# A gated recurrence over 512 steps: regrouping the recurrent product's PSUM banks, and dealing out the input products as 8, 8, 8, 4

## The chip, the core and the metric

The kernel runs on one core of a Trainium2 chip. The metric is the device time of one execution in microseconds (us), the median over several runs. Engines are named as in the profile: PE (TensorE, matmuls) and PEld (its loads of the stationary operand), DVE (VectorE), ACT (ScalarE), POOL (GpSimd), SP (SyncE, which issues DMAs).

## The reference, cut to what matters

```python
xT = jnp.swapaxes(x, 0, 1)                      # x: (8, 512, 512) = (batch, step, feature)

def step(h, x_t):                               # h: (8, 512)
    fused = jax.nn.sigmoid(jnp.concatenate([x_t, h], axis=-1) @ w_W + w_b)
    hidden_state, output_state = jnp.split(fused, 2, axis=-1)
    memory_state = x_t @ wx_W + wx_b + hidden_state * (h @ wh_W + wh_b)
    h_new = output_state * h + (1.0 - output_state) * jnp.tanh(memory_state)
    return (h_new, h_new)
_, hs = jax.lax.scan(step, h0, xT)
return x + jnp.swapaxes(hs, 0, 1)
```

Everything is float32. Each of the 512 steps multiplies the state of 8 x 512 numbers with 512 x 1536 weights: 512 columns for the gate `hidden_state` (called r in the kernel), 512 for `output_state` (z), and 512 for `h @ wh_W` (called h or hh). The input's share, x_t with 512 x 1536 weights too, doesn't depend on the state and can be made ahead.

## The kernel before

**Layout.** The state stands with the 512 features on partitions, in four chunks of 128 (k = 0 to 3). Chunks 0 and 1 are half A (tiles `hTA`), chunks 2 and 3 half B (`hTB`). In a matmul the state is the stationary operand, 32 columns wide (8 batch rows of the present step and 24 zeros), and the weights are the moving one. The output is 32 partitions high, so four matmuls with j = 0 to 3 stand side by side in the array, one to each group of 32 columns of it. The profile writes this as 128\*32. A float32 matmul of the program is two PE instructions.

**A step on PE.** Four steps are a group (`g = i // 4`, `s = i % 4`). The banks of PSUM, two sets of R, G and H, 128 columns each, are filled ahead with bias and input products, and the steps of a group add the recurrent product to 8 of 32 rows each. R holds r of both halves, G holds hh and z of half A, H holds z and hh of half B. The order is written out by hand (line 27): `R0 R1 G0 G1 R2 R3 G2 G3 H0 H1 H2 H3`. A unit such as R0 is the bank with the chunk k of the state, and it is four program matmuls, one for each j. Units with k = 0 and 1 need the new half A, those with k = 2 and 3 the new half B. What stands between two steps is input products (line 349).

**Input products.** Those of a pair of groups, eight steps, are 56 matmuls with 192 columns (`products`, line 288; they are 56, not 64, because sums of x and differences of weights are shared between the two groups). From step 5 on, every step takes seven of them after its H3. Since seven is not a multiple of four, three column groups get two and one gets one. `turn` (lines 343 and 350) carries on with the j that is next, so that the column group with one product is the first of the next step's R0, and each has its turn once in four steps. They run out with step 500: the last eleven steps have none.

**From PSUM to the next state** (lines 423 to 442), in DVE's order:

- `turn_r(0)`, `turn_r(1)`: transposes of R, 32x32 blocks, out of PSUM into `tr`; ACT makes r from each (`md0A`, `md0B`).
- `turn_h(0)`, `turn_z(0)`: the same for the two halves of G, into `md1A` and `tz`. `turn_z(0)` is made to wait for r of half A, so that the scans behind it need no wait of their own. ACT makes 1 - z (`hd0A`).
- `memory(0)`: two scans, one for each chunk of the half, make x_t wx + r (h wh) (`m`), and after each ACT makes tanh, into `hTA`.
- `update(0)`: two scans make the new half A (`hTA` of the next step), which PE waits for.
- `turn_h(1)`, `turn_z(1)`, `memory(1)`, `update(1)`: the same for half B, out of H.

After that follow, off this chain: copies of the state by ACT, `turn_x` (a transpose of the input's share for a later group), `spread` (ACT's copies of input products into a bank that is free), the copies and sums that finish the input products, three small memsets, and POOL's additions of x for the output, which SP stores after every 16 steps.

**Queues.** Each engine runs its instructions in the order in which the program issues them. On PE, the loads of stationary operands run ahead of the matmuls. The first load of R0, R1, R2 and R3 waits for DVE's scans.

Of the kernel before, what the change touches and what calls it, by code (L numbers as in the profile page):

```python
# [7 lines left out]
F32 = mybir.dt.float32  # L8
BF16 = mybir.dt.bfloat16
AF = mybir.ActivationFunctionType  # L10
ALU = mybir.AluOpType
PSUM = bass.MemoryType.PSUM

P = 128
NQ = 4
GS = 4
B = 8
HU = 64
# [5 lines left out]
LAST = 4  # L24
SYNC = mybir.DependencyInfo(mybir.DependencyClass.Sync, mybir.DependencyReason.DATA)

ORDER = "R0 R1 G0 G1 R2 R3 G2 G3 H0 H1 H2 H3"

FIRST = "Q0 x Q1 x Q2 x Q3 H0 H1 H2 H3"

BANKS = ("R", "G", "H")

HALF = 192

AL, BE = (0, slice(64, 256)), (0, slice(256, 448))
GA, DE = (1, slice(64, 256)), (1, slice(256, 448))

XP = {"G": slice(0, 128), "R": slice(128, 256), "X": slice(256, 384), "H": slice(384, 512)}


@with_exitstack
def tile_cond_rnn_residual(
# [2 lines left out]
    x: bass.AP,  # L45
    xh: bass.AP,
    wx_d: bass.AP,
    wgr_d: bass.AP,
    whh_d: bass.AP,
    wh3_d: bass.AP,  # L50
    bias_d: bass.AP,
    out: bass.AP,
    TC: int,
# [28 lines left out]
    nc = tc.nc  # L82
    NCH = x.shape[0]
    T = NCH * TC
    NG = T // GS
# [38 lines left out]
    for k in range(NQ):  # L124
        nc.sync.dma_start(out=wx[:, k], in_=wx_d[k])

    wgr = const.tile([P, NQ, NQ, 256], F32, name="wgr")
    for k in range(NQ):
        nc.sync.dma_start(out=wgr[:, k], in_=wgr_d[k])
    whh = const.tile([P, NQ, NQ, 128], F32, name="whh")  # L130
    nc.sync.dma_start(out=whh[:, :3], in_=whh_d)
    nc.sync.dma_start(out=whh[:, 3], in_=wh3_d)

    def wh(bank, k, j):
        return whh[:, k, j] if bank == "H" else wgr[:, k, j, {"G": slice(0, 128), "R": slice(128, 256), "Q": slice(0, 256)}[bank]]

    load_x(0, 1)

# [36 lines left out]
    def state(hf, i, slot=2):  # L175

        s = i % GS
        return hT[hf][i % NH][:, B * s : B * s + B, :, slot]

    ctx.enter_context(tc.manual_schedule())  # L180
    banks = [
        {n: psum.tile([P, 128], F32, name=f"{n}{q}") for n in BANKS}
        for q in range(2)
    ]
    xps = [psum.tile([P, 512], F32, name=f"xp{q}") for q in range(2)]
# [1 line left out]
    def mm(out_, lhsT, rhs, start=False):  # L187
        nc.tensor.matmul(  # L188
            out_, lhsT, rhs, start=start, stop=False, skip_group_check=True
        )  # L190


    for t_ in list(banks[0].values()) + list(banks[1].values()):
        mm(t_, none[:, :128], none, start=True)
    def warm():

        mm(xps[1], zeros[:, :128], zeros)
# [6 lines left out]
    for hf in range(2):  # L204
        for slot in (0, 2):
            nc.vector.tensor_copy(
                state(hf, 0, slot), hin[:, 2 * hf : 2 * hf + 2].rearrange("p c b -> p b c")
            )
    turn = [0]

# [2 lines left out]
    def act(key, out_, in_, func, **kw):  # L215
        inst = nc.scalar.activation(out_, in_, func, **kw).ins  # L216
        if key in written:
            tc.declare_no_dep(inst, written[key], reason="ordered through VectorE")
        written[key] = inst
        return inst  # L220
# [17 lines left out]
    def late(g):  # L238

        if g == 0:  # L240
            return xps[0][:, 256:512]
        return even if g % 2 == 0 else odd[g // 2 % 2]

    def spread(g, names):

        for n in names:
            src = late(g)[:, 128:256] if n == "H" else xps[g % 2][:, XP[n]]
            nc.scalar.copy(banks[g % 2][n], src)

    def turn_x(g, e):  # L250

        nc.vector.transpose(
            md1[e // 2][g % 2][:, :, e % 2, 1], late(g)[:, 32 * e : 32 * e + 32]
        )

    def reg(r):
        return xps[r[0]][:, r[1]]
# [47 lines left out]
    def take(it, n=None):  # L305
        while n is None or n > 0:
            if next(it, it) is it:
                return
            n = None if n is None else n - 1
# [9 lines left out]
    first = {g: prefill(g) for g in (1, 2, 3)}  # L319
    weight_sum(0)  # L320
    weight_sum(2)
    spread(0, "RGH")
    for e in range(NQ):
        turn_x(0, e)

# [1 line left out]
    for i in range(T):  # L327
# [7 lines left out]

        for n in (ORDER if i else FIRST).split():
            if n == "x":
                take(first[1], 1)
                continue
            bank, k = n[0], int(n[1])  # L340
            hs = hT[k // 2][i % NH][:, :, k % 2, 2]
            for j in range(NQ):
                j = (j + turn[0]) % NQ
                to = xps[0][:, :256] if bank == "Q" else ps[bank]
                mm(to[32 * j : 32 * j + 32, :], hs, wh(bank, k, j))
        if i < 5:
            take(first[(i + 3) // 2], 2)
        else:
            take(later, 7)
            turn[0] += 7  # L350

        rows = slice(B * s, B * s + B)

        def scans(hf, out_, d0, d1):

            for c_ in (slice(0, 1), slice(1, 2)):
                nc.vector.tensor_tensor_scan(  # L357
                    *[t_[:, :, c_].rearrange("p n c s -> p (n c s)") for t_ in (out_, d0, d1)],
                    0.0,
                    ALU.mult,  # L360
                    ALU.add,
                )
                yield c_

        if i:
            pg, pr = ps["G"], ps["R"]
        else:
            pg, pr = (xps[0][:, XP[n]] for n in "GR")
        raw = {
            "h": (pg[:, :HU], ps["H"][:, HU:]),  # L370
            "z": (pg[:, HU:], ps["H"][:, :HU]),
            "r": (pr[:, :HU], pr[:, HU:]),
        }

        def turned(n, hf):
            t_ = work.tile([P, 2, 32], F32, tag=f"t{n}{hf}", name=f"t{n}{hf}_{i}")
            inst = nc.vector.transpose(t_.rearrange("p c n -> p (c n)"), raw[n][hf]).ins  # L377
            return t_[:, :, rows], inst
# [1 line left out]
        r_done = [None, None]  # L380

        def turn_r(hf):
            tr, inst = turned("r", hf)

            if hf == 1 and i + 1 - NH in pool_done:
                tc.add_manual_dep(inst, pool_done[i + 1 - NH].name, SYNC)
            r_done[hf] = act(
                ("r", hf, g % 2, s),
                md0[hf][g % 2][:, rows, :, 1].rearrange("p n c -> p c n"),
                tr,  # L390
                AF.Sigmoid,
            )

        def turn_h(hf):
            nc.vector.transpose(  # L395
                md1[hf][g % 2][:, :, :, 0].rearrange("p n c -> p c n"), raw["h"][hf]
            )

        def turn_z(hf):
            tz, inst = turned("z", hf)  # L400

            tc.add_manual_dep(inst, r_done[hf].name, SYNC)
            act(
                ("zc", hf, i % 2),
                hd0[hf][i % 2][:, :, :, 2].rearrange("p n c -> p c n"),
                tz,
                AF.Sigmoid,
                scale=-1.0,
            )

        def memory(hf):

            m = work.tile([P, 2, B, 2], F32, tag=f"m{hf}", name=f"m{hf}_{i}").rearrange("p c n s -> p n c s")
            for c_ in scans(hf, m, md0[hf][g % 2][:, rows], md1[hf][g % 2][:, rows]):
                act(("n", hf, c_.start, i % NH), state(hf, i, 1)[:, :, c_], m[:, :, c_, 1], AF.Tanh)

        def update(hf):
            s1 = (i + 1) % GS
            new = hT[hf][(i + 1) % NH][:, B * s1 : B * s1 + B]
            for _ in scans(hf, new, hd0[hf][i % 2], hT[hf][i % NH][:, rows]):  # L420
                pass

        turn_r(0)
        turn_r(1)
        turn_h(0)
        turn_z(0)
        memory(0)
        update(0)
        if i == 0:

            seed(2)
        if i == T - 1:
# [3 lines left out]
                state(0, T),  # L436
                ALU.add,
            )
        turn_h(1)
        turn_z(1)  # L440
        memory(1)
        update(1)
        for hf in range(2):
            act(("h", hf, (i + 1) % NH), state(hf, i + 1, 0), state(hf, i + 1), AF.Copy)
        if i < 3:
# [3 lines left out]
        nxt, two = o + 1 < NG // 2, o + 2 < NG // 2  # L449
        if i == 0:  # L450
            nc.scalar.copy(odd[0], xps[1][:, 256:512])
        if g + 1 < NG:
            turn_x(g + 1, s)
        if i == 0:
            spread(1, "R")
        if u == 0:
            spread(2 * o + 1, "G")
            if o and nxt:
                nc.scalar.copy(reg(GA), reg(BE))
        elif u == 1:  # L460
            spread(2 * o + 1, "H")
        elif u == 2 and o == 0:
            seed(3)
            nc.scalar.copy(even, xps[0][:, 256:512])
        elif u == 2 and nxt:
            last = odd[(o + 1) % 2][:, :HALF]
            nc.vector.tensor_tensor(last, reg(GA), both, ALU.add)
        elif u == 3 and nxt:
            if o:
                nc.vector.tensor_tensor(even[:, :HALF], reg(BE), both, ALU.add)  # L470
            spread(2 * o + 2, "R")
        elif u == 4 and nxt:
            if o == 0:
                nc.scalar.copy(odd[1], xps[1][:, 256:512])
            spread(2 * o + 2, "G")
            if two:
                nc.scalar.copy(reg(AL), bias[:, AL[1]])
                x_sum(o + 2, 0)
        elif u == 5 and nxt:
            spread(2 * o + 2, "H")  # L480
            if two:
                nc.scalar.copy(reg(DE), step_bias)
                x_sum(o + 2, 1)
        elif u == 6 and two:
            nc.scalar.copy(reg(BE), reg(AL))
            x_sum(o + 2, 2)
        elif u == 7 and nxt:
            spread(2 * o + 3, "R")
            if two:
                nc.scalar.copy(both, reg(DE))  # L490
                x_sum(o + 2, 3)
# [104 lines left out]
```

## Time and profile before

| | us |
|---|---|
| median of 3 runs (lowest, highest) | 1681.29 (1680.15, 1682.52) |
| the profiled execution: its time | 1682.46 |
| the profiled execution: its span | 1679.9 |
| PE busy, PEld busy | 1668.8, 1645.4 |
| DVE busy, ACT busy, POOL busy | 1144.5, 947.4, 303.5 |
| granted PE clock, mean | 0.999 of full speed |

The span is what the profile covers; 2.6 us of the execution's time lie around it. A group of instructions is a row with line, engine, operation, what it writes and reads, its shape and its count, then its busy time and the mean of one in ns, then the idle time of its engine just before. A row of the timeline starts with the start in us from the beginning of the span and the length of the row, and several equal instructions that overlap stand in one row (x16). Line 188 is the helper `mm`, so PE's work is told apart by tiles. Matmuls overlap in the array, four at a time here, so PE's busy time has no gap where a single column group waits.

### The profile page before, as it was taken

What the parts mean: (1) busy time and instruction counts of PE and PEld (TensorE: products, weight loads), DVE (VectorE), ACT (ScalarE), POOL (GpSimd) and SP (SyncE); (2) the same over time, 40 slices, a digit from 0 to 9 for tenths busy, and PEclk for the clock granted to TensorE, in tenths of its full rate; (3) what the DMA queues carried; (4) which work ended last, traced back from release to release, by engine and by line L of the source; (5) the groups of instructions that cost most, each with busy time, mean ns of one, the idle gap of its engine ahead of it and who ended that gap; (6) DMA issues with size and microseconds to landing.
All of it is one profiled execution on the core that took longest, in us unless ns stands there. A gap on an engine that the chain in (4) does not pass through costs nothing.

```text
span 1679.9 us, 129621 instructions
## 1 busy us (share of the span) xinstructions
PE 1668.8 (99%) x56206; PEld 1645.4 (98%) x56206; DVE 1144.5 (68%) x9387; ACT 947.4 (56%) x5822; POOL 303.5 (18%) x1281
## 2 busy tenths in 40 slices
PE   8999999999999999999999999999999999999998
PEld 5999999999999999999999999999999999999997
DVE  6766666666666666666666666666666666666666
ACT  3555555555555555555555555555555555555554
POOL 1111111111111111111111111111111111111111
PEclk9999999999999999999999999999999999999999
DMA  4000000000000000000000000000000000000000
GB/s 178 17 5 17 18 18 17 17 5 18 17 18 18 5 17 18 17 17 5 18 18 17 18 15 7 18 17 17 17 5 18 17 18 17 5 18 12 11 11 10
DMA packets 11523, 31.37 MB, mean 19 GB/s; under 512 B 1220, under 2 KB 1732, under 8 KB 10952
## 3 DMA queue, kind: packets, MB, share of 16 engines
q1 hardware_dynamic: 10800, 22.94, 3.9%
q8 instruction: 439, 7.19, 1.7%
q14 instruction: 132, 1.08, 0.2%
q10 hardware_dynamic: 152, 0.16, 0.0%
HBM read 14.70 MB, written 8.39 MB: 14 GB/s over the span
## 4 chain that ended last, share of the span: by engine, by line
PE 99%; DVE 1%; DMA 0%; ACT 0%; issue 0%
PE R L188 27%; PE G L188 26%; PE H L188 26%; PE xp L188 19%; DMA rows<-in_bias_dram 0%; DVE md1A L395 0%; DVE hTA L357 0%; ACT hd0A L216 0%; DVE tz L377 0%; ACT hTA L216 0%; DVE bias L203 0%; DVE rows L120 0%; ACT hTB L216 0%; DVE hTB L357 0%; ACT hd0B L216 0%
## 5 line engine op out<-in xcount | busy, mean ns | idle before, releaser
L188 PE MATMUL R<-wgr,hTA 128*32 128x128 f32 x8176 | 431.5, 275 | 2.4 <-DVE hTA L357 2.2
L188 PE MATMUL G<-wgr,hTA 128*32 128x128 f32 x8176 | 411.9, 273 | 0.0
L377 DVE STREAM_TRANSPOSE tr<-R 128x64 f32<-128x64 f32 x1022 | 194.4, 228 | 286.9 <-PE R L188 286.8
L188 PE MATMUL R<-wgr,hTB 128*32 128x128 f32 x8176 | 385.9, 275 | 0.0
L499 POOL TENSOR_TENSOR ot<-xin,hTB 128x16 f32<-128x16 f32 x503 | 126.6, 252 | 1331.5 <-DVE hTB L357 1323.4
L188 PE MATMUL H<-whh,hTB 128*32 128x128 f32 x8192 | 366.4, 273 | 0.0
L188 PE MATMUL H<-whh,hTA 128*32 128x128 f32 x8192 | 366.2, 273 | 0.0
L188 PE MATMUL G<-wgr,hTB 128*32 128x128 f32 x8176 | 365.5, 273 | 0.0
L188 PEld LDWEIGHTS G<-wgr,hTA 128*32 128x32 f32 x8176 | 334.5, 122 | 0.2
L188 PEld LDWEIGHTS R<-wgr,hTA 128*32 128x32 f32 x8176 | 301.2, 123 | 9.0 <-DVE hTA L357 5.5
L188 PEld LDWEIGHTS H<-whh,hTB 128*32 128x32 f32 x8192 | 289.0, 122 | 0.1
L188 PEld LDWEIGHTS H<-whh,hTA 128*32 128x32 f32 x8192 | 289.0, 122 | 0.1
L188 PEld LDWEIGHTS G<-wgr,hTB 128*32 128x32 f32 x8176 | 288.6, 122 | 0.0
L216 ACT ACTIVATE hd0B<-tz 128x16 f32<-128x16 f32 x512 | 116.5, 228 | 279.4 <-DVE tz L377 279.3
L188 PEld LDWEIGHTS R<-wgr,hTB 128*32 128x32 f32 x8176 | 255.2, 123 | 2.2 <-DVE hTB L357 0.5
L216 ACT ACTIVATE md0A<-tr 128x16 f32<-128x16 f32 x512 | 112.0, 219 | 237.5 <-DVE tr L377 237.4
L188 PE MATMUL xp<-tw,sx 128*32 128x192 f32 x2976 | 229.3, 326 | 0.0
L357 DVE TENSOR_TENSOR_SCAN hTB<-hd0B,hTB 128x24 f32<-128x24 f32 x1024 | 158.0, 196 | 104.6 <-ACT hTB L216 104.4
L357 DVE TENSOR_TENSOR_SCAN hTA<-hd0A,hTA 128x24 f32<-128x24 f32 x1024 | 157.7, 195 | 103.2 <-ACT hTA L216 103.2
L188 PE MATMUL xp<-wx,xin 128*32 128x192 f32 (+1 forms) x2048 | 178.2, 331 | 0.4 <-issue 0.4
L216 ACT ACTIVATE hd0A<-tz 128x16 f32<-128x16 f32 x512 | 115.7, 226 | 111.1 <-DVE tz L377 111.1
L216 ACT ACTIVATE hTB<-hTB 128x16 f32<-128x16 f32 x512 | 120.4, 235 | 79.6 <-DVE hTB L357 70.9
(90 smaller groups left out, 2408.9 us busy)
## 6 DMA issues: line engine op xcount, KB each, us to landing
xin<-in_x_dram SPq DMA_DIRECT2D x31, 256.0 KB, 3.5
out_dram<-ot SPq DMA_DIRECT2D x31, 256.0 KB, 2.2
wx<-in_wx_dram SPq DMA_DIRECT2D x4, 768.0 KB, 7.0
wgr<-in_wgr_dram SPq DMA_DIRECT2D x4, 512.0 KB, 9.7
whh<-in_whh_dram SPq DMA_DIRECT2D x1, 768.0 KB
whh<-in_wh_dram SPq DMA_DIRECT2D x1, 256.0 KB, 10.9
out_dram<-ot SPq DMA_DIRECT2D x1, 192.0 KB, 1.8
head<-in_xh_dram ACTq DMA_DIRECT2D x1, 144.0 KB, 5.0
```

Of the source, the lines that this page charges most:

```text
L188: nc.tensor.matmul(out_, lhsT, rhs, start=start, stop=False, skip_group_check=True)
L216: inst = nc.scalar.activation(out_, in_, func, **kw).ins
L357: nc.vector.tensor_tensor_scan(*[t_[:, :, c_].rearrange("p n c s -> p (n c s)") for t_ in (out_, d0, d1)], 0.0, ALU.mult, ALU.add,)
L377: inst = nc.vector.transpose(t_.rearrange("p c n -> p (c n)"), raw[n][hf]).ins
L499: return engine.tensor_tensor(ot[:, t, 2 * hf : 2 * hf + 2, :].rearrange("p c n -> p n c"), x_of(c, slice(2 * hf, 2 * hf + 2), t, 1).rearr ...
```

## The change

The banks are now A (192 columns: hh, z and r of half A), B (128: r and hh of half B) and C (64: z of half B). The order of a step becomes `A0 B0 A1 A2 A3 B1 B2 B3 C0 C1 C2 C3`. `turn` is gone; a step takes eight input products, and only four if it is the first of its group. On DVE, `turn_r(1)`, `turn_h(1)` and `turn_z(1)` move in between the scans of half A, and the second `update` of half A comes after them; it waits for r of half B. What waited for POOL's additions was `turn_r(1)`, and is now `turn_h(0)`. `turn_x` runs up to four steps later and reads partly from PSUM. The columns of the weights and of `wx` are regrouped to fit, in the host's code and in the loads: `wa` (four loads of 384 KB) and `wb` (one of 1152 KB and one of 384 KB) in place of `wgr` (four of 512 KB) and `whh` (768 and 256 KB).

```diff
-ORDER = "R0 R1 G0 G1 R2 R3 G2 G3 H0 H1 H2 H3"
-FIRST = "Q0 x Q1 x Q2 x Q3 H0 H1 H2 H3"
-BANKS = ("R", "G", "H")
+ORDER = "A0 B0 A1 A2 A3 B1 B2 B3 C0 C1 C2 C3"
+FIRST = "A0 x A1 x A2 x A3 B0 B1 B2 B3 C0 C1 C2 C3"
+BANKS = {"A": 192, "B": 128, "C": 64}
...
-XP = {"G": slice(0, 128), "R": slice(128, 256), "X": slice(256, 384), "H": slice(384, 512)}
+XP = {"A": slice(0, 192), "X": slice(192, 320), "C": slice(320, 384), "B": slice(384, 512)}
...
+    def part(g, c0, c1):
+        return late(g)[:, c0 - 256 : c1 - 256] if c0 >= 256 else xps[g % 2][:, c0:c1]
     def spread(g, names):
         for n in names:
-            src = late(g)[:, 128:256] if n == "H" else xps[g % 2][:, XP[n]]
-            nc.scalar.copy(banks[g % 2][n], src)
+            nc.scalar.copy(banks[g % 2][n], part(g, XP[n].start, XP[n].stop))
     def turn_x(g, e):
-        nc.vector.transpose(
-            md1[e // 2][g % 2][:, :, e % 2, 1], late(g)[:, 32 * e : 32 * e + 32]
-        )
+        c0 = XP["X"].start + 32 * e
+        nc.vector.transpose(md1[e // 2][g % 2][:, :, e % 2, 1], part(g, c0, c0 + 32))
...
             for j in range(NQ):
-                j = (j + turn[0]) % NQ
-                to = xps[0][:, :256] if bank == "Q" else ps[bank]
+                to = ps[bank] if i or bank != "A" else xps[0][:, XP["A"]]
                 mm(to[32 * j : 32 * j + 32, :], hs, wh(bank, k, j))
         if i < 5:
             take(first[(i + 3) // 2], 2)
         else:
-            take(later, 7)
-            turn[0] += 7
+            take(later, 8 if s else 4)
...
         raw = {
-            "h": (pg[:, :HU], ps["H"][:, HU:]),
-            "z": (pg[:, HU:], ps["H"][:, :HU]),
-            "r": (pr[:, :HU], pr[:, HU:]),
+            "h": (pa[:, :HU], ps["B"][:, HU:]),
+            "z": (pa[:, HU : 2 * HU], ps["C"]),
+            "r": (pa[:, 2 * HU :], ps["B"][:, :HU]),
         }
...
         def turn_z(hf):
             tz, inst = turned("z", hf)
-            tc.add_manual_dep(inst, r_done[hf].name, SYNC)
+            if hf == 0:
+                tc.add_manual_dep(inst, r_done[0].name, SYNC)
...
         turn_r(0)
-        turn_r(1)
         turn_h(0)
         turn_z(0)
-        memory(0)
-        update(0)
+        memory(0, 0)
+        memory(0, 1)
+        turn_r(1)
+        update(0, 0)
+        turn_h(1)
+        turn_z(1)
+        tc.add_manual_dep(update(0, 1), r_done[1].name, SYNC)
...
-        turn_h(1)
-        turn_z(1)
-        memory(1)
-        update(1)
+        memory(1, 0)
+        memory(1, 1)
+        update(1, 0)
+        update(1, 1)
...
-        if g + 1 < NG:
-            turn_x(g + 1, s)
+        ahead = 2 * o + (1 if u < 3 else 2 if u < 7 else 3)
+        if ahead < NG:
+            turn_x(ahead, (u + 1) % GS)
         if u == 0:
-            spread(2 * o + 1, "G")
+            spread(2 * o + 1, "B")
...
```

In the calls of `spread`, R, G and H become A, B and C step for step.

More of the change, by code (lines that the diff above doesn't have):

```diff
@@ L47, in tile_cond_rnn_residual @@
     wx_d: bass.AP,
-    wgr_d: bass.AP,
-    whh_d: bass.AP,
-    wh3_d: bass.AP,
+    wa_d: bass.AP,
+    wb_d: bass.AP,
+    wb3_d: bass.AP,
     bias_d: bass.AP,
@@ L125, in tile_cond_rnn_residual @@
         nc.sync.dma_start(out=wx[:, k], in_=wx_d[k])
-    wgr = const.tile([P, NQ, NQ, 256], F32, name="wgr")
+    wa = const.tile([P, NQ, NQ, 192], F32, name="wa")
     for k in range(NQ):
[L129 to L132, printed above, removed]
+        nc.sync.dma_start(out=wa[:, k], in_=wa_d[k])
+    wb = const.tile([P, NQ, NQ, 192], F32, name="wb")
+    nc.sync.dma_start(out=wb[:, :3], in_=wb_d)
+    nc.sync.dma_start(out=wb[:, 3], in_=wb3_d)
     def wh(bank, k, j):
-        return whh[:, k, j] if bank == "H" else wgr[:, k, j, {"G": slice(0, 128), "R": slice(128, 256), "Q": slice(0, 256)}[bank]]
+        return wa[:, k, j] if bank == "A" else wb[:, k, j, {"C": slice(0, 64), "B": slice(64, 192)}[bank]]
     load_x(0, 1)
@@ L181, in tile_cond_rnn_residual @@
     banks = [
-        {n: psum.tile([P, 128], F32, name=f"{n}{q}") for n in BANKS}
+        {n: psum.tile([P, w], F32, name=f"{n}{q}") for n, w in BANKS.items()}
         for q in range(2)
@@ L193, in tile_cond_rnn_residual @@
     for t_ in list(banks[0].values()) + list(banks[1].values()):
-        mm(t_, none[:, :128], none, start=True)
+        mm(t_, none, none[:, :1].broadcast_to([P, t_.shape[1]]), start=True)
     def warm():
@@ L208, in tile_cond_rnn_residual @@
             )
-    turn = [0]
     written = {}
@@ L321, in tile_cond_rnn_residual @@
     weight_sum(2)
-    spread(0, "RGH")
+    spread(0, "BCA")
     for e in range(NQ):
@@ L348, in tile_cond_rnn_residual, with scan @@
         else:
-            take(later, 7)
-            turn[0] += 7
+            take(later, 8 if s else 4)
         rows = slice(B * s, B * s + B)
[L354 to L368, printed above, removed]
+        def scan(c_, out_, d0, d1):
+            return nc.vector.tensor_tensor_scan(
+                *[t_[:, :, c_].rearrange("p n c s -> p (n c s)") for t_ in (out_, d0, d1)],
+                0.0,
+                ALU.mult,
+                ALU.add,
+            ).ins
+        pa = ps["A"] if i else xps[0][:, XP["A"]]
         raw = {
-            "h": (pg[:, :HU], ps["H"][:, HU:]),
-            "z": (pg[:, HU:], ps["H"][:, :HU]),
-            "r": (pr[:, :HU], pr[:, HU:]),
+            "h": (pa[:, :HU], ps["B"][:, HU:]),
+            "z": (pa[:, HU : 2 * HU], ps["C"]),
+            "r": (pa[:, 2 * HU :], ps["B"][:, :HU]),
         }
@@ L382, in turn_r @@
         def turn_r(hf):
-            tr, inst = turned("r", hf)
-            if hf == 1 and i + 1 - NH in pool_done:
-                tc.add_manual_dep(inst, pool_done[i + 1 - NH].name, SYNC)
+            tr, _ = turned("r", hf)
             r_done[hf] = act(
@@ L394, in turn_h @@
         def turn_h(hf):
-            nc.vector.transpose(
+            inst = nc.vector.transpose(
                 md1[hf][g % 2][:, :, :, 0].rearrange("p n c -> p c n"), raw["h"][hf]
-            )
+            ).ins
+            if hf == 0 and i + 1 - NH in pool_done:
+                tc.add_manual_dep(inst, pool_done[i + 1 - NH].name, SYNC)
         def turn_z(hf):
             tz, inst = turned("z", hf)
-            tc.add_manual_dep(inst, r_done[hf].name, SYNC)
+            if hf == 0:
+                tc.add_manual_dep(inst, r_done[0].name, SYNC)
             act(
@@ L409, in turn_z, with memory, update @@
             )
[L411 to L417, printed above, removed]
+        ms = [
+            work.tile([P, 2, B, 2], F32, tag=f"m{hf}", name=f"m{hf}_{i}").rearrange("p c n s -> p n c s")
+            for hf in range(2)
+        ]
+        def memory(hf, q):
+            c_ = slice(q, q + 1)
+            scan(c_, ms[hf], md0[hf][g % 2][:, rows], md1[hf][g % 2][:, rows])
+            act(("n", hf, q, i % NH), state(hf, i, 1)[:, :, c_], ms[hf][:, :, c_, 1], AF.Tanh)
+        def update(hf, q):
             s1 = (i + 1) % GS
             new = hT[hf][(i + 1) % NH][:, B * s1 : B * s1 + B]
-            for _ in scans(hf, new, hd0[hf][i % 2], hT[hf][i % NH][:, rows]):
-                pass
+            return scan(slice(q, q + 1), new, hd0[hf][i % 2], hT[hf][i % NH][:, rows])
         turn_r(0)
-        turn_r(1)
         turn_h(0)
         turn_z(0)
-        memory(0)
-        update(0)
+        memory(0, 0)
[5 more added lines that the diff above has]
+        tc.add_manual_dep(update(0, 1), r_done[1].name, SYNC)
         if i == 0:
@@ L451, in tile_cond_rnn_residual @@
             nc.scalar.copy(odd[0], xps[1][:, 256:512])
-        if g + 1 < NG:
-            turn_x(g + 1, s)
-        if i == 0:
-            spread(1, "R")
+            spread(1, "A")
+            turn_x(1, 0)
+        ahead = 2 * o + (1 if u < 3 else 2 if u < 7 else 3)
+        if ahead < NG:
+            turn_x(ahead, (u + 1) % GS)
         if u == 0:
-            spread(2 * o + 1, "G")
+            spread(2 * o + 1, "B")
             if o and nxt:
@@ L460, in tile_cond_rnn_residual @@
         elif u == 1:
-            spread(2 * o + 1, "H")
+            spread(2 * o + 1, "C")
         elif u == 2 and o == 0:
@@ L470, in tile_cond_rnn_residual @@
                 nc.vector.tensor_tensor(even[:, :HALF], reg(BE), both, ALU.add)
-            spread(2 * o + 2, "R")
+            spread(2 * o + 2, "A")
         elif u == 4 and nxt:
@@ L474, in tile_cond_rnn_residual @@
                 nc.scalar.copy(odd[1], xps[1][:, 256:512])
-            spread(2 * o + 2, "G")
+            spread(2 * o + 2, "B")
             if two:
@@ L479, in tile_cond_rnn_residual @@
         elif u == 5 and nxt:
-            spread(2 * o + 2, "H")
+            spread(2 * o + 2, "C")
             if two:
@@ L487, in tile_cond_rnn_residual @@
         elif u == 7 and nxt:
-            spread(2 * o + 3, "R")
+            spread(2 * o + 3, "A")
             if two:
@@ L551 @@
     w, wxm, whm = f["L0_cond_w_W"], f["L0_cond_wx_W"], f["L0_cond_wh_W"]
-    wb, wxb, whb = f["L0_cond_w_b"], f["L0_cond_wx_b"], f["L0_cond_wh_b"]
+    wb_, wxb, whb = f["L0_cond_w_b"], f["L0_cond_wx_b"], f["L0_cond_wh_b"]
     def quads(a):
@@ L565, in chunks @@
         return c_(units(a).swapaxes(0, 1))
-    wx_d = chunks(cat((z[:D], half_a), (r[:D], both), (wxm, both), (z[:D], half_b)))
-    wgr_d = chunks(cat((whm, half_a), (z[D:], half_a), (r[D:], both)))
-    wh = units(cat((z[D:], half_b), (whm, half_b)))
-    whh_d, wh3_d = c_(wh[:, :3]), c_(wh[:, 3])
-    rb, zb = wb[:512], wb[512:]
-    bias_d = c_(cat((whb, half_a), (zb, half_a), (rb, both), (wxb, both), (zb, half_b), (whb, half_b))[0])
+    wx_d = chunks(cat((z[:D], half_a), (r[:D], half_a), (wxm, both), (z[:D], half_b), (r[:D], half_b)))
+    wa_d = chunks(cat((whm, half_a), (z[D:], half_a), (r[D:], half_a)))
+    wb = units(cat((z[D:], half_b), (r[D:], half_b), (whm, half_b)))
+    wb_d, wb3_d = c_(wb[:, :3]), c_(wb[:, 3])
+    rb, zb = wb_[:512], wb_[512:]
+    bias_d = c_(
+        cat((whb, half_a), (zb, half_a), (rb, half_a), (wxb, both), (zb, half_b), (rb, half_b), (whb, half_b))[0]
+    )
     xd = units(_np.moveaxis(x, 2, 0))
@@ L582 @@
     for name, a in (
-        ("x", xd), ("xh", xh_d), ("wx", wx_d), ("wgr", wgr_d), ("whh", whh_d), ("wh3", wh3_d), ("bias", bias_d),
+        ("x", xd), ("xh", xh_d), ("wx", wx_d), ("wa", wa_d), ("wb", wb_d), ("wb3", wb3_d), ("bias", bias_d),
     ):
```

## The prediction

> **What bounds the kernel now.** I read the page first.
>
> ```profile
> span 1679.9 us, 129621 instructions
> PE 1668.8 (99%) x56206; PEld 1645.4 (98%) x56206; DVE 1144.5 (68%) x9387; ACT 947.4 (56%) x5822; POOL 303.5 (18%) x1281
> ...
> PE 99%; DVE 1%; DMA 0%; ACT 0%; issue 0%
> ```
>
> PE never stands still as a whole, but four column groups work in it, and one can wait unseen. So I went to the timeline of the last steps, which have no input products, and where the chain from PSUM to the next state lies bare. One step, on DVE:
>
> ```profile
> 1655.62 0.38 DVE L377 STREAM_TRANSPOSE tr<-R 128x64 f32<-128x64 f32 x2 [0.55 <-PE R L188]
> 1656.06 0.25 DVE L395 STREAM_TRANSPOSE md1A<-G 128x64 f32<-128x64 f32 x1
> 1656.23 0.21 DVE L377 STREAM_TRANSPOSE tz<-G 128x64 f32<-128x64 f32 x1
> 1656.36 0.26 DVE L357 TENSOR_TENSOR_SCAN m<-md0A,md1A 128x16 f32<-128x16 f32 x2
> 1656.82 0.31 DVE L357 TENSOR_TENSOR_SCAN hTA<-hd0A,hTA 128x24 f32<-128x24 f32 x2 [0.20 <-ACT hTA L216]
> 1657.05 0.22 DVE L395 STREAM_TRANSPOSE md1B<-H 128x64 f32<-128x64 f32 x1
> 1657.20 0.20 DVE L377 STREAM_TRANSPOSE tz<-H 128x64 f32<-128x64 f32 x1
> ...
> 1659.21 0.25 DVE L395 STREAM_TRANSPOSE md1A<-G 128x64 f32<-128x64 f32 x1
> ```
>
> on ACT (r, 1 - z, tanh of half A):
>
> ```profile
> 1655.90 0.22 ACT L216 ACTIVATE md0A<-tr 128x16 f32<-128x16 f32 x1 [0.53 <-DVE tr L377]
> ...
> 1656.47 0.23 ACT L216 ACTIVATE hd0A<-tz 128x16 f32<-128x16 f32 x1 [0.22 <-DVE tz L377]
> 1656.60 0.29 ACT L216 ACTIVATE hTA<-m 128x8 f32<-128x8 f32 x2
> ```
>
> and on PE, with the loads of R's first units:
>
> ```profile
> 1657.09 0.66 PE L188 MATMUL R<-wgr,hTA 128*32 128x128 f32 x16 [0.22 <-DVE hTA L357]
> ...
> 1658.53 0.62 PE L188 MATMUL G<-wgr,hTB 128*32 128x128 f32 x16
> 1658.96 0.62 PE L188 MATMUL H<-whh,hTA 128*32 128x128 f32 x16
> ```
> ```profile
> 1657.08 0.19 PEld L188 LDWEIGHTS R<-wgr,hTA 128*32 128x32 f32 x8 [0.48 <-DVE hTA L357]
> ```
>
> To be seen: without input products the loop takes 1659.21 - 1656.06 = 3.15 us; half A's scan starts at 1656.82, PE's loads 0.26 later; and R's row is 0.66 long where G's is 0.62, so a load that had to wait costs 0.04. With products I count turns of G:
>
> ```profile
> L395 DVE STREAM_TRANSPOSE md1A<-G 128x64 f32<-128x64 f32 x464 | 117.8, 254 | 26.1
> L188 PE MATMUL xp<-tw,sx 128*32 128x192 f32 x2976 | 229.3, 326 | 0.0
> L188 PE MATMUL G<-wgr,hTA 128*32 128x128 f32 x8176 | 411.9, 273 | 0.0
> ```
>
> The first row is of the window from 100 to 1600 us: 1500 / 464 = 3.233 us a step, 12.93 for four.
>
> **PE's share, in us.** Sixteen instructions (two units) start 0.43 to 0.44 apart (1658.53, 1658.96), four in each column group: 0.109 each. 192 columns last 326 - 273 = 0.053 longer: 0.162. A unit is two instructions in each column group, so 0.218 with 128 columns and 0.325 with 192. Twelve units make 2.62; a product adds 0.325 to its column group.
>
> Before, a column group thus needs 2.62 + 0.65 = 3.27 in three steps of four, and 2.95 in the one in which it gets one product and leads. There it waits for the loop. I take the 3.15 to 3.16 of the tail less 0.04, since there all four column groups start again late and apart, and here one. 3 x 3.27 + 3.12 = 12.93, as counted. So the kernel is bound by PE in three steps of four, and by the loop in the fourth; without any wait four steps would take 4 x 2.62 + 28 / 4 x 0.325 = 12.76.
>
> **The change, part by part.**
>
> *Widths.* The columns are the same: 4 x 0.325 + 4 x 0.218 + 4 x 0.112 = 2.62. The 0.112 for C is a straight line downwards, 0.109 - 0.053 = 0.056 an instruction; no row has 64 columns. Bounds: 0.056, and 0.109 if a narrow one cost what 128 columns do. I take 0.056: a waiting load costs 0.04 (R's 0.66 against 0.62), less than 0.056, and eight loads fit into 0.19 with 0.12 for each (mean 123 ns), (0.19 - 0.12) / 7 = 0.01 apart; C needs one every 0.014. The Trainium skill speaks against it: "TensorE: Matmul & The Clock Gate", section "LDWEIGHTS (loading the stationary operand)", has a load last its columns over 1.2 GHz, 27 ns for 32. One after another, that would make C's 32 loads a step 0.85 instead of 0.45, and the time some 0.4 x 500 = 200 us longer. The loads 0.01 apart in the row above speak for loads that overlap, and my sum goes without it.
>
> *Products.* 28 in four steps as before. All column groups now get two, or all get one: PE asks for 3.27, 3.27, 3.27 and 2.95, and no column group runs ahead.
>
> *Half A's chain.* Time 0 is the start of B1 in the last column group, where A ends. A's last instruction still has 0.273 - 0.109 = 0.16 to run, and DVE starts 0.04 to 0.06 later (in the tail G ends at 1658.53 + 0.62 = 1659.15 and its turn starts at 1659.21): `turn_r(0)` at 0.20 to 0.23. r was ready early; now r, hh and z end together, and `turn_z(0)` must wait for ACT's r: 0.28 (1655.62 to 1655.90) + 0.22 + 0.03 from ACT to DVE (tanh from 1656.60, 0.20 long, scan at 1656.82) = 0.53, where two transposes alone would take 0.17 each. From there as before: z's turn to half A's first scan is 1656.82 - 1656.23 = 0.59, and to the loads 0.26. Loads at 0.20 + 0.53 + 0.85 = 1.58 to 1.61, matmul 0.04 later: 1.62 to 1.65.
> PE gets to A0 after B1 to B3, C and products: 3 x 0.218 + 0.447 + 0.65 = 1.75, the first column group 0.02 earlier. No wait there. With four products it gets there at 1.43, and waits about 0.2.
>
> *Half B's chain.* After half A's first scan (0.20 + 1.12 = 1.32 to 1.35): `turn_h(1)` + 0.10 (1656.82, a second scan 0.13 later, 1657.05), `turn_z(1)` + 0.15, second scan + 0.13, m's scan + 0.10 to 0.13, tanh + 0.21 (m's mean of 0.17 and 0.03 to 0.04 to ACT), scan + 0.23, loads + 0.26. Sum 1.18 to 1.21: loads at 2.50 to 2.56, matmul at 2.54 to 2.60, last column group 0.02 later. If z's turn takes longer after standing idle (the two turns of `tr` last 0.38 with starts 0.17 apart: 0.25 for a first, 0.21 for the second), 0.04 more: 2.56 to 2.66 in all. PE gets to A2 at 1.75 + 0.325 + 0.218 + 0.325 = 2.62. With A2 and A3 (0.65) the next time 0 comes at 3.27 to 3.31 in a step with eight, and at 3.21 to 3.31 in one with four, where PE alone would need 2.95. Four steps: 13.02 to 13.24, against 12.93: + 0.09 to 0.31. With the loop in the middle, 3.26, they take 3 x 3.27 + 3.26 = 13.07; as a loop above 3.27 lengthens all four steps and one below it only one, I take 13.09, + 0.16.
>
> *Ends.* Steps 5 to 500 are 124 times four: + 11 to 38 us, taken + 20. The last eleven pay 0.06 to 0.16 each: + 1 to 2. The first five have 384-column products that hide all this.
>
> *Costed at nothing.* `spread` copies the same columns, `turn_x` moves within DVE's order, the wait for POOL is for an addition seven steps old; DVE idles 0.55 a step before `tr`, ACT 0.53, and that is their cover; without it each would cost its 0.19 to 0.27 in the step concerned. `turn_r(1)` falls into DVE's idle 0.20 before half A's scans, and B's bank is done by then (0.65 + 0.2 = 0.85, asked for at 1.05); so is C's (about 1.3, asked for at 1.57). B0 and C0 wait for turns that are over by 1.9, and start after 1.95. SP's loads for step 0: 5.6 MB instead of 5.8 stand ahead of B0; below 0.5 once.
>
> Sum: 1682.46 (the profiled execution, span 1679.9 and 2.6 around it) + 21 = 1704. The median shown is 1.2 lower, which makes **1703**.
>
> **Rivals.**
>
> *Faster: the end of A comes earlier.* A is done after 4 x 0.325 + 0.218 = 1.52 of a step, G was after 8 x 0.218 = 1.75. If r stayed off the path (z's turn 0.35 behind r's, not 0.53), both loads come 0.18 earlier, a step with four takes 3.03 to 3.13 and four steps 12.84 to 12.94, 12.89 in the middle: 1681 - 5 = 1676. With no wait anywhere, 12.76: 1681 - 21 = 1660. It decides from 12.93 = 9.81 + 3.12: the loop has to be under 3.12. For it: the 0.23 are real. Against: m's scan needs r whatever the order, and r's 0.53 is in the rows.
>
> *Slower by far: narrow matmuls.* If C's instructions cost 0.109, every step pays 8 x 0.053 = 0.42, also behind the loop's waits in most: 3 x 3.70 + 3.37 = 14.47, + 191 us, about 1873. It leaves the main case's range from 0.063 an instruction on (3 x 8 x 0.007 x 124 = 21 on top of 1703). For it: no row has 64 columns. Against: the loads.
>
> *No change.* Should the step with four take 3.12 by other small savings, 1681.
>
> **How the numbers follow.** Main case 0.78; faster 0.10; none 0.04; narrow matmuls 0.08. This kernel's three runs lie within 0.07% of their median, so 0.2% tells a change. Main case's range is 1693 to 1721 (+ 12 to + 40 on 1681); the rivals outside it hold 0.2, and the range given is 1690 to 1722. Slower: 0.78 + 0.08 = 0.86.
>
> **What would show it.** The turn of A's r, once a step: intervals of 3.27 to 3.31 in three and 3.21 to 3.31 in the fourth. ACT's r ahead of z's turn in every step, DVE idle for about 0.2 between `turn_h(0)` and `turn_z(0)`. PE idle, or its A0 waiting for `hTA`, only behind four products. C's 32 instructions within 0.45. I am wrong if four steps take under 12.93, if the step with four takes under 3.12, or if C takes 0.5 or more.

## The result and the profile after

The changed kernel takes 1720.37 us (median of 4 runs, 1719.41 to 1723.04) against 1681.9 before: a ratio of 1.0231, 95% interval 1.0213 to 1.0249. It is slower, as forecast, and near the far end of the range: 38 us more where 21 were taken. The profiled execution took 1723.04 us, 1720.5 of them in its span. From its page (a group's last numbers are busy time, mean ns of one, and the engine's idle time ahead of them):

```profile
span 1720.5 us, 129875 instructions
PE 1698.3 (99%) x56238; PEld 1414.3 (82%) x56238; DVE 1126.3 (65%) x9387; ACT 959.0 (56%) x5822; POOL 303.1 (18%) x1281
...
PE 88%; DVE 6%; ACT 4%; issue 1%; DMA 0%
...
L188 PEld LDWEIGHTS A<-wa,hTB 128*32 128x32 f32 x8176 | 243.6, 125 | 111.5 <-DVE hTB L355 92.3
...
L371 DVE STREAM_TRANSPOSE tz<-A 128x64 f32<-128x64 f32 x511 | 128.0, 251 | 79.0 <-ACT md0A L215 75.9
```

PE's busy share is 99% in both kernels, because one matmul or another is always under way. What tells them apart is the loads, busy for 82% of the span instead of 98%, and the chain that ended last, which before was PE to 99% and now goes through DVE and ACT too. Of the idle time of the loads, 92.3 us are laid to half B's scan, ahead of A2. z's turn waits 76 us for ACT's r.

One step on DVE in the changed kernel's timeline:

```profile
808.10 0.25 DVE L371 STREAM_TRANSPOSE tr<-A 128x64 f32<-128x64 f32 x1 [0.76 <-PE A L188]
808.28 0.21 DVE L386 STREAM_TRANSPOSE md1A<-A 128x64 f32<-128x64 f32 x1
808.64 0.25 DVE L371 STREAM_TRANSPOSE tz<-A 128x64 f32<-128x64 f32 x1 [0.16 <-ACT md0A L215]
...
809.27 0.21 DVE L355 TENSOR_TENSOR_SCAN hTA<-hd0A,hTA 128x24 f32<-128x24 f32 x1
...
810.20 0.31 DVE L355 TENSOR_TENSOR_SCAN hTB<-hd0B,hTB 128x24 f32<-128x24 f32 x2 [0.19 <-ACT hTB L215]
...
811.41 0.25 DVE L371 STREAM_TRANSPOSE tr<-A 128x64 f32<-128x64 f32 x1 [0.76 <-PE A L188]
```

and on PE and its loads:

```profile
808.51 0.41 PE L188 MATMUL C<-wb,hTA 128*32 128x64 f32 x16
808.73 0.41 PE L188 MATMUL C<-wb,hTB 128*32 128x64 f32 x16
808.95 0.83 PE L188 MATMUL xp<-wx,xin 128*32 128x192 f32 x16
...
810.47 0.87 PE L188 MATMUL A<-wa,hTB 128*32 128x192 f32 x16
```
```profile
810.47 0.51 PEld L188 LDWEIGHTS A<-wa,hTB 128*32 128x32 f32 x16 [0.17 <-DVE hTB L355]
```

The loop is 811.41 - 808.10 = 3.31 us. It goes 0.54 from r's turn to z's, 0.63 to half A's scan, 1.20 to the loads for A2, and 0.94 from there over A2 and A3 to the next turn. This step has eight products (the sixteen instructions at 808.95) and is no exception. The table has the median interval between one step's turn and the next one's, by the step that it starts from, over steps 13 to 490, and in the last steps, where there are no products; the turn is that of hh of half A. It holds most of the runs told of below, too.

| us | after s = 0 | s = 1 | s = 2 | s = 3 | last steps |
|---|---|---|---|---|---|
| before | 3.247 | 3.252 | 3.253 | 3.207 | 3.158 |
| changed | 3.309 | 3.306 | 3.308 | 3.307 | 3.302 |
| changed, r of A from a constant | 3.006 | 3.270 | 3.270 | 3.270 | 3.007 |
| changed, seven products a step | 3.308 | 3.305 | 3.305 | 3.305 | 3.303 |
| changed, wait on r ahead of the scan | 3.152 | 3.271 | 3.271 | 3.270 | 3.150 |
| before, with 8, 8, 8, 4 | 3.162 | 3.270 | 3.270 | 3.270 | 3.157 |
| before, z with r first | 3.233 | 3.253 | 3.249 | 3.219 | 3.148 |
| before, hh with r first, z last | 3.239 | 3.245 | 3.189 | 3.242 | 3.068 |

In the changed kernel all steps take the same, with eight products, four or none. PE binds none of them.

### The profile page after: what moved, and what is told of

The parts are those of the page before. It is cut to its first block, busy times and chain, and to the rows that moved or that the text cites. A ratio compares the mean times of both kernels' runs of the same rounds, so it can differ in the third digit from the quotient of the medians.

```text
span 1720.5 us, 129875 instructions
## 1 busy us (share of the span) xinstructions
PE 1698.3 (99%) x56238; PEld 1414.3 (82%) x56238; DVE 1126.3 (65%) x9387; ACT 959.0 (56%) x5822; POOL 303.1 (18%) x1281
## 4 chain that ended last, share of the span: by engine, by line
PE 88%; DVE 6%; ACT 4%; issue 1%; DMA 0%
PE A L188 42%; PE B L188 21%; PE xp L188 15%; PE C L188 10%; DVE tz L371 2%; DVE tr L371 2%; ACT md0A L215 2%; ACT hd0A L215 2%; DVE hTA L355 2%; ACT hTA L215 1%; DMA rows<-in_bias_dram 0%; DVE bias L203 0%; ACT hTB L215 0%; ACT xp L223 0%; DVE rows L120 0%
## 5 line engine op out<-in xcount | busy, mean ns | idle before, releaser
L188 PE MATMUL A<-wa,hTA 128*32 128x192 f32 x8176 | 527.3, 329 | 13.3 <-DVE hTA L355 4.0
L188 PE MATMUL A<-wa,hTB 128*32 128x192 f32 x8176 | 446.2, 335 | 0.2 <-DVE hTB L355 0.2
L188 PE MATMUL B<-wb,hTA 128*32 128x128 f32 x8192 | 414.0, 273 | 0.0
L188 PEld LDWEIGHTS A<-wa,hTB 128*32 128x32 f32 x8176 | 243.6, 125 | 111.5 <-DVE hTB L355 92.3
L188 PEld LDWEIGHTS B<-wb,hTA 128*32 128x32 f32 x8192 | 292.8, 121 | 40.9
L188 PEld LDWEIGHTS A<-wa,hTA 128*32 128x32 f32 x8176 | 236.2, 123 | 109.4 <-DVE hTA L355 61.6
L188 PE MATMUL B<-wb,hTB 128*32 128x128 f32 x8192 | 318.7, 273 | 0.0
L188 PEld LDWEIGHTS B<-wb,hTB 128*32 128x32 f32 x8192 | 241.4, 122 | 0.0
L188 PE MATMUL C<-wb,hTA 128*32 128x64 f32 x8192 | 209.4, 219 | 0.0
L188 PE MATMUL C<-wb,hTB 128*32 128x64 f32 x8192 | 209.3, 219 | 0.0
```

The lines of the kernel that those rows point to most:

```text
L188: nc.tensor.matmul(out_, lhsT, rhs, start=start, stop=False, skip_group_check=True)
```

## The experiments

The theory is that every step of the changed kernel is bound by the loop from bank A's end over r, z's turn, the scans and half B back to A. The rivals: PE pays for the regrouped widths, or the dealing of the products costs. The kernel before ran beside each on the same chip.

### r of half A taken off the path

```diff
-            "r": (pa[:, 2 * HU :], ps["B"][:, :HU]),
+            "r": (bias[:, :HU], ps["B"][:, :HU]),
```

> The changed kernel, with r of half A made from a constant in SBUF instead of from bank A, so that its turn and ACT's r are done long before half A's turns and z's turn has nothing to wait for. Left out: the gate r of half A (its work on DVE and ACT stays). Theory (every step is bound by the loop from the end of A over r, z's turn, the scans and half B back to A): z's turn comes 0.17 us behind the first turn instead of 0.53, and without idle time before it, so the loop falls from 3.31 to 2.88 to 2.95 us; four steps take 12.76 (PE's own work) to 12.85, and the time is 1655 to 1672 us. Rival (PE pays for the regrouped widths or for the dealing 8, 8, 8, 4): PE's work is the same, so the time stays within 10 us of 1720.

Measured: 1669.42 us, ratio to before 0.9925 (0.991 to 0.994). On DVE:

```profile
809.15 0.25 DVE L386 STREAM_TRANSPOSE md1A<-A 128x64 f32<-128x64 f32 x1 [0.70 <-PE A L188]
809.33 0.21 DVE L371 STREAM_TRANSPOSE tz<-A 128x64 f32<-128x64 f32 x1
...
809.92 0.21 DVE L355 TENSOR_TENSOR_SCAN hTA<-hd0A,hTA 128x24 f32<-128x24 f32 x1
...
810.89 0.31 DVE L355 TENSOR_TENSOR_SCAN hTB<-hd0B,hTB 128x24 f32<-128x24 f32 x2 [0.20 <-ACT hTB L215]
...
812.16 0.25 DVE L386 STREAM_TRANSPOSE md1A<-A 128x64 f32<-128x64 f32 x1 [0.67 <-PE A L188]
```

and on PE:

```profile
811.15 0.87 PE L188 MATMUL A<-wa,hTB 128*32 128x192 f32 x16
```

z's turn is 0.18 behind the first instead of 0.54, half A's scan 0.59 behind that instead of 0.63. PE's work is untouched, and 51 us are gone against the changed kernel. The steps with eight products are at PE's own 3.27, and the one with four at a loop of 3.01, not the 2.88 to 2.95 of the expectation. Of the 0.40 that z's turn and half A's scan gain, some 0.1 is lost again: half B's scan comes 0.97 behind half A's instead of 0.93, and the next step's first turn starts 0.14 behind the end of A's last matmuls (811.15 + 0.87 = 812.02, 812.16) instead of 0.07 (810.47 + 0.87 = 811.34, 811.41). What makes these two later, no run here shows. PE and its new widths aren't the cause of the longer time; r's way over DVE and ACT is.

### Seven products a step again

```diff
-            take(later, 8 if s else 4)
+            take(later, 7)
+            turn[0] += 7
```

(and `j = (j + turn[0]) % NQ` as before)

> The changed kernel, with the input products dealt out as before: seven in every step, and the order of the column groups carried on. Theory (loop-bound in every step): the loop stays at 3.26 to 3.31 us whoever leads, and the time is 1700 to 1722 us. Rival (the step with only four products is what costs): PE asks for 3.19 a step on the mean and the time falls back to 1680 to 1690 us.

Measured: 1719.06 us, ratio 1.0222 (1.0207 to 1.0237). The dealing is not what costs: undoing it gives back nothing that the runs' spread would show.

### The same dealing, in the kernel before

```diff
-                j = (j + turn[0]) % NQ
...
-            take(later, 7)
-            turn[0] += 7
+            take(later, 8 if s else 4)
```

> The kernel before, with its input products dealt out as 8, 8, 8, 4 and the column groups always in the order 0 to 3. Theory: its loop is 3.12 to 3.16 us, so four steps take 3 x 3.27 + 3.12 to 3.16 = 12.93 to 12.97, and the time is 1681 to 1687 us. Rival (the dealing costs 0.3 us in four steps by itself): 1715 us or more.

Measured: 1686.67 us, ratio 1.0028 (1.0017 to 1.0039). Its row in the table has the form of the sum that was written for the kernel before: three steps at PE's 3.270 and one at the loop, 3.162, where 3.12 to 3.16 was expected. The new dealing by itself costs some 5 us here, not the 38 of the change.

### Leaving the products out

```diff
-            take(later, 8 if s else 4)
+            pass
```

> The changed kernel without any input product from step 5 on. Left out: the input's share of all later groups, so 28 of 220 matmuls in four steps. Theory: the loop binds every step, with or without products, and leaving them out saves nothing: 1712 to 1722 us. Rival (PE binds the three steps with eight products): they get shorter by up to 0.65 us each, below 1500 us in all.

Measured, by a single run: 1717.12 us, and intervals of 3.302 to 3.307. Of PE's own 12.76 us in four steps 3 x 0.65 + 0.325 = 2.27 are gone, and the time is 0.2% below the changed kernel's. What binds is not the sum of PE's work, though A2 and A3 are a part of the loop.

### The wait moved behind z's turn

```diff
-            if hf == 0:
-                tc.add_manual_dep(inst, r_done[0].name, SYNC)
...
-        turn_h(0)
         turn_z(0)
+        turn_h(0)
+        gate = nc.vector.memset(idle[:, :1], 0.0).ins
+        tc.add_manual_dep(gate, r_done[0].name, SYNC)
         memory(0, 0)
```

> The changed kernel, with z's turn ahead of hh's and no wait on r before either; a memset of one column behind them waits for r, in front of the first scan. Theory (r's 0.53 us and then z's turn and ACT's 1 - z in a row make the loop): tanh follows the scan 0.21 us behind r instead of waiting for z, at 0.77 us behind the first turn instead of 0.94, so the loop is 3.12 to 3.16; the steps with eight products become PE-bound at 3.27, four steps take 12.93 to 12.97, and the time is 1680 to 1688 us. Rival (PE pays): no change from 1720 us. A second rival (the loop is half B's alone, behind bank C): no change either, since B's and C's ends stay where they are.

Measured: 1686.59 us, ratio 1.0031 (1.0018 to 1.0044). On DVE:

```profile
810.16 0.25 DVE L371 STREAM_TRANSPOSE tr<-A 128x64 f32<-128x64 f32 x1 [0.64 <-PE A L188]
...
810.47 0.21 DVE L386 STREAM_TRANSPOSE md1A<-A 128x64 f32<-128x64 f32 x1
810.71 0.19 DVE L355 TENSOR_TENSOR_SCAN m<-md0A,md1A 128x16 f32<-128x16 f32 x1
...
811.18 0.21 DVE L355 TENSOR_TENSOR_SCAN hTA<-hd0A,hTA 128x24 f32<-128x24 f32 x1
```

The scan of memory comes 0.55 behind r's turn, as r's own length asks for, and half A's scan 1.02 behind it, not 1.17. That is 0.15 off the loop, and 34 us off the time. It shows that the order on DVE decided, with every bank and every matmul left as the change made them. The second rival, half B behind bank C, falls too: B and C end as before. With this order repaired, the changed kernel takes what the kernel before takes with the same dealing (1686.59 and 1686.67 us): in kernels that PE binds in three steps of four, the rest of the change neither costs nor gains on balance.

### r of half A in columns of its own

```diff
+ORDER = "R0 A0 B0 R1 A1 R2 R3 A2 A3 B1 B2 B3 C0 C1 C2 C3"
+BANKS = {"A": 128, "B": 128, "C": 128}
...
+        if n in "CR":
+            return banks[q]["C"][:, :HU] if n == "C" else banks[q]["C"][:, HU:]
```

> The changed kernel, with r of half A in 64 columns of its own that are finished 0.44 us ahead of hh and z of half A (order R0 A0 B0 R1 A1 R2 R3 A2 A3, then B and C; R shares a bank with C). Theory: r is off the loop, which falls to 2.95 to 3.03 us as in the run with a constant r; PE pays 0.02 a step for 16 more instructions. Four steps take 3 x 3.29 + 2.97 to 3.03 = 12.84 to 12.90, and the time is 1669 to 1677 us. Rival (r made from a constant was fast for another reason, such as a turn that doesn't read PSUM): 1700 us or more.

Measured: 2367.58 us, ratio 1.4074 (1.4051 to 1.4098). That is over the rival's 1700 too, but neither theory nor rival had the reason. From the groups on PE:

```profile
L190 PE MATMUL C<-wa,hTA 128*32 128x64 f32 x8176 | 321.5, 229 | 566.8 <-DVE tz L379 459.4 <-DVE hTA L363 107.4
```

and one turn of r on DVE:

```profile
1203.74 0.25 DVE L379 STREAM_TRANSPOSE tr<-C 128x64 f32<-128x64 f32 x1 [2.09 <-PE C L190]
```

R0 of a step waits for the turn of z of half B, which reads the other half of the same tile, and r's turn in its place waits for C's matmuls. With these waits in the way the run says nothing of the theory. That the shared tile makes them is read from the rows and not shown by a second run: a tile of its own for R wasn't tried.

### What leaves PE first: z with r

If the loop is what binds, the kernel before should gain from a shorter one as well, in its fourth step. First try: z and r of half A in the first bank, hh of A and r of B in the second.

```diff
-            "z": (pg[:, HU:], ps["H"][:, :HU]),
-            "r": (pr[:, :HU], pr[:, HU:]),
+            "z": (pr[:, :HU], ps["H"][:, :HU]),
+            "r": (pr[:, HU:], pg[:, HU:]),
...
         turn_r(0)
-        turn_r(1)
-        turn_h(0)
         turn_z(0)
+        turn_h(0)
+        gate = nc.vector.memset(idle[:, :1], 0.0).ins
+        tc.add_manual_dep(gate, r_done[0].name, SYNC)
         memory(0)
+        turn_r(1)
```

> The kernel before, with two columns groups exchanged: its first bank holds z and r of half A, its second hh of half A and r of half B; DVE turns r and z of half A first, then hh, a memset waits for r, and r of half B is turned behind the scans of memory. Order on PE, dealing of the products and number of instructions are those of before. Theory (what ACT has to work on must leave PE first, and the step that leads is bound by the loop): the scan follows hh's turn directly and tanh no longer waits for 1 - z, so half A's scans come 0.15 us earlier; half B's turns then wait for bank H and gain 0.11; the loop falls from 3.12 to 2.96 to 3.04 us, four steps take 12.77 to 12.85, and the time is 1658 to 1670 us. Rival (the kernel before is bound by PE alone): 1680 us or more.

Measured: 1681.06 us, ratio 0.9998 (0.9989 to 1.0007): no change. On DVE:

```profile
801.39 0.25 DVE L395 STREAM_TRANSPOSE md1A<-G 128x64 f32<-128x64 f32 x1
801.60 0.06 DVE L427 MEMSET idle<- 128x1 f32 x1
801.67 0.28 DVE L357 TENSOR_TENSOR_SCAN m<-md0A,md1A 128x16 f32<-128x16 f32 x2
...
802.15 0.31 DVE L357 TENSOR_TENSOR_SCAN hTA<-hd0A,hTA 128x24 f32<-128x24 f32 x2
```

r was ready before (ACT's row for it is 801.24 and 0.22 long), but the scan reads what hh's turn has just written, and comes 0.28 behind it, with only the one-column memset between; before, z's turn stood between the two. Half A's scan is again 0.76 behind hh's turn (1656.82 - 1656.06 = 0.76 before).

### What leaves PE first: hh with r, and z last

So the turn that comes last should be one that the scan of memory doesn't read:

```diff
-            "h": (pg[:, :HU], ps["H"][:, HU:]),
-            "z": (pg[:, HU:], ps["H"][:, :HU]),
-            "r": (pr[:, :HU], pr[:, HU:]),
+            "h": (pr[:, :HU], ps["H"][:, HU:]),
+            "z": (pg[:, :HU], ps["H"][:, :HU]),
+            "r": (pr[:, HU:], pg[:, HU:]),
...
         turn_r(0)
-        turn_r(1)
         turn_h(0)
         turn_z(0)
+        gate = nc.vector.memset(idle[:, :1], 0.0).ins
+        tc.add_manual_dep(gate, r_done[0].name, SYNC)
         memory(0)
+        turn_r(1)
```

> The kernel before, with hh and r of half A in its first bank and z of half A with r of half B in the second: r has half a bank's time (0.44 us) ahead, and what comes last is z, which only the state's scan needs. DVE turns r, hh, then z; a memset waits for r in front of the scan of memory; r of half B is turned behind that scan. Theory: from the second bank's end to half A's scans it takes 0.28 to ACT's 1 - z, 0.12 to tanh, 0.23 to the scan, 0.63 us in all, where before it takes 0.76 to 0.77, and the RAW wait of 0.28 us between hh's turn and the scan that ate the gain of the last run is hidden behind z's turn. The loop falls from 3.15 to 3.02 to 3.05 us in the last steps, 0.04 less where one column group leads; four steps take 12.79 to 12.84 and the time is 1663 to 1670 us. Rival (half B's chain behind bank H binds, whatever half A does): 1679 to 1683 us, and a loop of 3.15 us in the last steps.

Measured: 1669.96 us, ratio 0.9928 (0.9915 to 0.9942), by 5 runs. On DVE:

```profile
801.06 0.25 DVE L377 STREAM_TRANSPOSE tz<-G 128x64 f32<-128x64 f32 x1
801.24 0.19 DVE L357 TENSOR_TENSOR_SCAN m<-md0A,md1A 128x16 f32<-128x16 f32 x1
...
801.71 0.31 DVE L357 TENSOR_TENSOR_SCAN hTA<-hd0A,hTA 128x24 f32<-128x24 f32 x2
```

From bank G's first turn (z's here, hh's before) to half A's scan it takes 0.65 instead of 0.76; the loop of the last steps is 3.07 where 3.02 to 3.05 was expected. This version beats both kernels: 0.7% faster than before, 2.9% faster than the change (1669.96 / 1720.37).

## Why the prediction was right, and where its size was off

- **What bounds the kernel before** (PE in three steps of four, the loop in the fourth): right for the sum of four steps, but other runs show it, not this kernel's own intervals, which are 3.21 to 3.25 and not 3.27 three times and 3.12. With the products dealt out evenly over the column groups, they are 3.270 three times and 3.162. And the version with z last has the order on PE and the dealing of before, and a loop that is 0.09 shorter in the last steps (3.068 for 3.158). It is 11.8 us faster than the kernel before beside it (1681.8); without the last eleven steps' 1.0 that is 0.09 in four steps (10.8 / 124), so the loop is paid for once in four steps.
- **Widths** at no cost, 0.056 for an instruction with 64 columns: right. C's sixteen start 0.22 apart (808.51, 808.73, 808.95), four to a column group, so 0.055 each. The rival of narrow matmuls falls with that. An estimate from the 27 ns a load of the Trainium skill ("TensorE: Matmul & The Clock Gate", section "LDWEIGHTS (loading the stationary operand)"), with one load after another, would have kept those sixteen 0.43 apart. The measured 0.22 decides for loads that overlap.
- **r on the path**, 0.53 from its turn to z's: right, 0.54. The rival with half A's earlier end falls: r puts z's turn 0.36 later than two turns in a row would (0.54 against 0.18), and the earlier end brings 0.23. The run with a constant r shows it from the other side: without r on the path the loop is 3.01.
- **Half B**, 1.18 to 1.21 from half A's scan to the loads: right, 1.20.
- **From z's turn to half A's scan**: mis-sized. 0.59 was taken from the row, with at most 0.04 for a turn after idle time, half of it in the sum; the trace has 0.63, and 0.59 again where z's turn doesn't stand idle first. A turn that waited costs all of it.
- **From the loads to the next turn**: 0.04 + 0.02 + 0.65 + 0.20 to 0.23 = 0.91 to 0.94, measured 0.94, the upper end.
- **The sum**: each term came out within 0.01 of its bounds, but all of them in the upper half: 3.31 where the bounds were 3.21 to 3.31 and 3.26 was taken. So the way of the loop was right, and what failed is taking it "in the middle". That the range still held the time is due to its upper end, where all terms are at their largest. Its price isn't even on both sides, as the prediction itself says: under 3.27 one step of four pays, over it all of them. 4 x 3.307 is 13.23, 0.30 over the 12.93 counted before, not 0.16; times 124 that makes 37 us, and the last steps another 11 x 0.144 = 1.6. Measured is 38.
- **What was to be seen**: the intervals came as written, and DVE idles 0.15 to 0.16 ahead of z's turn, where about 0.2 was written. Behind four products or none the loads of A wait for half A's scan, as forecast (61.6 us in 136 waits). Not forecast was that the loads for A2 wait for half B's scan in nearly every step (499 waits, 92.3 us), behind eight products too.
- **Costed at nothing**: the run with the wait moved has all the rest of the change in it and lies at the time of the kernel before with the same dealing, so these terms are nothing on balance. One of them was described wrongly: by the kernels' code `turn_x` runs one step earlier than before, not up to four steps later.

## What to carry to other kernels

In a recurrence, group the outputs by when the next step's chain asks for them, not by the half of the state to which they belong: what another engine must still work on leaves first, and what only the last operation reads may leave last. A busy engine that shows no idle time isn't proof of a bound if its work can overlap; leave some of its work out, and see whether the time moves. And where a loop lies just under another bound, the sum is not even around the middle: take each term's upper end before leaving the loop out of three steps in four.

## What the runs showed of the hardware

- Matmuls in different column groups start out of program order. In the trace of before, R's first starts at 800.41 and two of the input products, which stand ahead of it in the program, at 800.50 and 800.52; by the code R's first goes to the column group that has one product less. So PE as a whole doesn't keep to the order in which the program issues:

```profile
800.41 0.31 PE L188 MATMUL R<-wgr,hTA 128*32 128x128 f32 x1
800.50 0.34 PE L188 MATMUL xp<-wx,xin 128*32 128x192 f32 x2
```

- A scan that reads what the transpose ahead of it wrote, with no more than a one-column memset between, starts 0.03 us behind that transpose's end: 0.28 behind its start where it lasts 0.25 (801.39 to 801.67), 0.24 where it lasts 0.21 (810.47 to 810.71). With a transpose between that it doesn't read, it follows that one by 0.13 (1656.23 to 1656.36), before its end, and 0.30 behind the start of the one that it reads: the transpose between adds only 0.02.
- A DVE transpose out of PSUM that waited lasts 0.25 us, and one right behind another 0.21 (808.10 and 808.28 in the changed kernel). z's turn, which waits there, is one of the first kind (808.64), and half A's scan comes 0.63 behind it instead of 0.59.
- The load of a stationary operand with 32 columns shows as 0.12 us (mean 123 ns), but where it has to wait for the scan the row of sixteen matmuls behind it is only 0.04 longer: 0.66 against 0.62 with 128 columns, and 0.87 for A2 and A3 against 0.83 for products of the same 192 columns. Where it doesn't wait it adds nothing that shows, even with a matmul of 0.055 behind it.
